# A vision state-space layer between its scans: averages folded into the sums, weights applied early, a second set of PSUM buffers

## The chip, the cores and the metric

The kernel runs on one core of a Trainium2 chip. The metric is the device time of one execution in microseconds (us). A core has five engines that take part here: TensorE (PE in the profile; PEld is its loading of weights), VectorE (DVE), ScalarE (ACT), GpSimd (POOL) and SyncE (SP), which only issues transfers. Each engine works through its own list of instructions in order and waits for the others by semaphores.

## The reference, cut to what matters

The model has four layers on an image of 2 x 56 x 56 positions with 128 channels. Layers 0 and 1 are selective-scan layers, layers 2 and 3 are attention and a mixer or experts. The change concerns layer 1 and the first step of layer 2. Layer 1 cuts the 128 channels into four heads of 32 and treats one after the other, because each head needs the result of the one before:

```python
prev = _vss_block(chunks[0], p) + vss_skip * chunks[0]
outs = [prev]
for i in range(1, g):
    s = prev + chunks[i]
    prev = _vss_block(s, p) + vss_skip * s
    outs.append(prev)
x_cat = jnp.concatenate(outs, axis=3)
x_res = cvm_skip * x_orig + x_cat
return _layernorm(x_res, final_ln_w, final_ln_b)
```

A block is `x + _ss2d(_layernorm(x))`, and `_ss2d` is, with 64 inner channels:

```python
xx, z = jnp.split(x @ p['in_proj_w'].T, 2, axis=-1)
xx = silu(depthwise_conv3x3(xx) + p['conv_b'])
# four scans over the positions: by rows, by columns, and both backwards;
# each: h = exp(dt*A)*h + dt*x*B ; y = sum over 16 states of h*C, plus x*Ds
y = y_rows + y_rows_back + y_columns + y_columns_back
y = _layernorm(y, p['out_norm_w'], p['out_norm_b']) * jax.nn.silu(z)
return y @ p['out_proj_w'].T
```

Layer 2 begins with `t = t + attention(_ln_t(t))`, a normalisation of the 128 channels of each position.

## The kernel before, in words

Two layouts are used. In "channels" layout the partitions are channels: layer 1 puts the 64 inner channels of both images side by side on 128 partitions, with 3136 positions along the free axis. In "tokens" layout 112 positions lie on the partitions; the tile `X` holds all positions and channels so. A chunk is 448 positions, four tiles of 112; there are 7 chunks (`NCH`).

**Scans.** `Scans.run` handles one head. Its order is written out by hand, step by step (`emit`). A step is one state of one quarter of the positions in one direction: ScalarE computes the decay (L334), VectorE the product `h` (L412) and the scan (L353), GpSimd the product `p` with C (L425), and TensorE adds the `p` of all 16 states into the PSUM tile `acc` (`add_up`, L373), multiplying by the identity matrix. `begin_sum` starts `acc` with the skip term (`skips`, a diagonal matrix) or with what the earlier directions left in `y`; ScalarE copies `acc` into `y` (L393).

**Between scans.** From one head to the next, and after the last, `Layer1.run` goes through the chunks. In this part the program text does not fix the order: a scheduler places the instructions of all chunks on each engine by when their inputs and buffers are free; pools give the number of buffers. For a chunk:

- `after` (the end of a head) calls `gated_tokens`: TensorE multiplies `y` by an averaging matrix into the PSUM tile `pm` (L486), VectorE subtracts it (L490), ScalarE squares (L492), GpSimd multiplies by the gate `z` (L494), TensorE forms the variance `pv` and the two output products `p1` (from the gated y) and `p2` (from the gate) (L504), ScalarE takes the root (L506), VectorE the reciprocal (L507). Then L861 and L862 combine the products, L863 on GpSimd adds the head's input, L864 adds the weighted input to give the new `prev`, and L866 adds the weighted original channels into `X`.
- `before` (the start of the next head) adds the next 32 channels to `prev` (L822), normalises (`layernorm_tokens`, L77 to L84, the last product on GpSimd), transposes on TensorE (L830), copies (L831), multiplies by the input weights (L833, L845), writes the padded image `pad` (L834) and the gate `z` with Silu (L846). `conv_rows` does the 3x3 convolution of the chunk before, on TensorE for even-numbered rows of chunks (18 matmul instructions, L455) or on VectorE (L459, L461), Silu on ScalarE (L462) and a GpSimd copy into column order (L463). At chunk 2 the first quarter of the next scans is prepared (`Scans.first`): row products, Softplus, and a way through DRAM in four transfers issued by SP.
- After the last head, `last` normalises `X` over 128 channels and applies weight and bias on GpSimd (L876), and `Attention2.chunk` normalises again (tiles `U`, `stu`), transposes for attention (L1102) and makes the value tiles (L1242).

The PSUM pool for the tiles of `after` and the transposes has one buffer per name, the one in `Attention2.start` two. ScalarE needs a table load (ACT_TABLE_LOAD) each time that its function changes among Sqrt, Silu, Exp and Softplus.

Of the kernel before, what the change touches and what calls it, by code (L numbers as in the profile page):

```python
# [21 lines left out]
B = 2  # L22
# [47 lines left out]

def layernorm_tokens(k, out, x, sq, st, d, by=None):


    nc = k.nc
    g = x.shape[1]
    mean, var = st[:, 0, :], st[:, 1, :] if by is None else by
    nc.vector.tensor_reduce(mean, x, AX.X, ALU.add)  # L77
    nc.vector.tensor_scalar_mul(mean, mean, 1.0 / d)
    nc.vector.tensor_tensor(out, x, mean.unsqueeze(2).to_broadcast([TP, g, d]), ALU.subtract)
    nc.scalar.activation(sq, out, AF.Square)  # L80
    nc.vector.tensor_reduce(var, sq, AX.X, ALU.add)
    nc.scalar.activation(var, var, AF.Sqrt, bias=k.eps[:TP], scale=1.0 / d)
    nc.vector.reciprocal(var, var)
    nc.gpsimd.tensor_tensor(out, out, var.unsqueeze(2).to_broadcast([TP, g, d]), ALU.mult)  # L84

# [20 lines left out]
class Scans:  # L106
# [263 lines left out]
    def add_up(self, x):  # L370
        nc, job, n = self.k.nc, x["job"], x["n"]
        for i in range(2):
            nc.tensor.matmul(  # L373
                job["acc"][:, i, 0:392], lhsT=self.k.ident, rhs=x["p"][:, 392 * i : 392 * (i + 1)],
                start=False, stop=n == NS - 1,
            )
# [138 lines left out]

def skips(k, pool, Ds, nch):

# [5 lines left out]
    for ci in range(nch):  # L523
        nc.vector.tensor_scalar_mul(out[:, ci], k.ident, total[:, ci : ci + 1])
    return out
# [28 lines left out]
def layer0(k, d, big, follow):  # L554
# [3 lines left out]
    with ExitStack() as ctx:  # L558
# [42 lines left out]
        with ExitStack() as sctx:  # L601
# [9 lines left out]
            sel = selection(k, wq, 1)  # L611
            skip = skips(k, wq, W["Ds"], 2)
            with k.pool("in0", 2) as ip, k.pool("pin0", 2, psum=True) as pp:
# [13 lines left out]
                "selB": lambda n: sel[:, n],  # L627
                "skip": lambda ci: skip[:, ci],
                "rows": 32,
                "rowC": 16,  # L630
# [96 lines left out]
class Layer1:  # L727
# [6 lines left out]
    def __init__(self, k, ctx, d, big):  # L734
# [20 lines left out]
        for n in ("vss_skip", "cvm_skip", "final_ln_w", "final_ln_b"):  # L755
            t = wp.tile([TP, d["L1_" + n].shape[0]], F32, name="L1" + n)
            nc.sync.dma_start(t, d["L1_" + n].partition_broadcast(TP))
            R[n] = t
        negative_exp(nc, W["A"])
        self.diag = wp.tile([128, 9, 128], F32, name="diag1")  # L760
        diagonals(k, self.diag, W["taps"])
        skip = skips(k, wp, W["Ds"].unsqueeze(2), 1)

        self.avg = wp.tile([128, 128], F32, name="avg1")
        nc.gpsimd.memset(self.avg, 0.0)
        nc.gpsimd.memset(self.avg[0:64, 0:64], 1.0 / 64)
        nc.gpsimd.memset(self.avg[64:128, 64:128], 1.0 / 64)
        self.mean = wp.tile([128, 2], F32, name="mean1")
# [4 lines left out]
        for n in ("onw", "onb"):  # L773
            t = wp.tile([128, B * D], F32, name="out" + n)
            nc.vector.tensor_scalar(t, W["out_w"], W[n], None, ALU.mult)
            self.outs.append([t])

# [5 lines left out]
        with k.pool("pinb", psum=True) as pp:  # L783
# [13 lines left out]
            "selB": lambda n: sel[:, n],  # L797
            "skip": lambda ci: skip[:, 0],
            "rows": 64,
            "rowC": 32,  # L800
# [9 lines left out]
    def before(self, head, pools, c, pad):  # L810
# [5 lines left out]
        if c < NCH:  # L816
# [9 lines left out]
            st = sp.tile([TP, 2, 4 * B], F32, name="st")  # L826
            layernorm_tokens(k, nv, sv, sq, st, D)
            pt = pp.tile([2 * D, CH], F32, name="pt")
            for i in range(4):
# [20 lines left out]
    def after(self, head, pools, c):  # L850
        k, nc, D, R = self.k, self.k.nc, self.D, self.R
        sp, pp = pools
        gate = [self.z[:, CH * c : CH * (c + 1)]]
        p1, p2, rs = gated_tokens(k, (sp, pp, sp), 1, [self.y], gate, self.avg, self.mean, *self.outs, c, B)
        t = sp.tile([TP, 4 * B, D], F32, name="t")

        def tokens(p):
            return p.rearrange("p j (b c) -> p (j b) c", c=D)

        s = self.chunk(self.prev, c)  # L860
        nc.vector.tensor_tensor(t, tokens(p1), rs.unsqueeze(2).to_broadcast([TP, 4 * B, D]), ALU.mult)  # L861
        nc.vector.tensor_tensor(t, t, tokens(p2), ALU.add)  # L862
        nc.gpsimd.tensor_tensor(t, t, s, ALU.add)  # L863
        nc.vector.scalar_tensor_tensor(s, s, R["vss_skip"], t, ALU.mult, ALU.add)  # L864
        xo = self.chunk(self.channels(head), c)
        nc.vector.scalar_tensor_tensor(xo, xo, R["cvm_skip"], s, ALU.mult, ALU.add)  # L866

    def last(self, sp, c):
# [4 lines left out]
        st = sp.tile([TP, 2, 4 * B], F32, name="stf")  # L873
        layernorm_tokens(k, xv, xv, sq, st, C)
        for op, n in ((ALU.mult, "final_ln_w"), (ALU.add, "final_ln_b")):
# [17 lines left out]
    def run(self, follow):  # L893
# [3 lines left out]
        for head in range(1, 5):  # L897
            self.scans.run()
            with ExitStack() as ctx:
                pp = ctx.enter_context(k.pool("pmid1", psum=True))  # L900
                if head < 4:
# [174 lines left out]
class Attention2:  # L1076
# [9 lines left out]
    def start(self, ctx):  # L1086
        self.sp = ctx.enter_context(self.k.pool("a2u", 2))
        self.pp = ctx.enter_context(self.k.pool("pa2", 2, psum=True))
        return self.chunk

    def chunk(self, c):
# [5 lines left out]
        flat = "p j b c -> p (j b) c"  # L1097
        layernorm_tokens(k, U.rearrange(flat), k.X[:, 4 * c : 4 * (c + 1)].rearrange(flat), sq, st, C)
        for b in range(B):
# [888 lines left out]
```

## Time and profile before

| what | us |
|---|---|
| median of 3 runs (9167.24 to 9182.95) | 9172.03 |
| profiled execution, its own time | 9196.55 |
| its span from first to last instruction | 9194.7 |
| TensorE busy in the span | 8062.6 |
| VectorE busy | 7113.2 |
| GpSimd busy | 6325.5 |
| ScalarE busy | 3845.9 |

Layer 1 lies between about 2880 and 5932 us of the span. A row of an answer gives start, length, engine, line and operation, the tiles written and read, and in square brackets the idle time before it and what ended that. A group row gives the number of instructions, the busy time and the mean length in ns. "Granted clock" is the TensorE clock in the records, 1 being full speed.

### The profile page before, as it was taken

How to read it: one execution, taken by the hardware profiler on the slowest of the kernel's cores; microseconds unless marked ns; L12 is line 12 of the kernel's file. 1: busy time of each engine (PE TensorE's matmuls, PEld its weight loads, DVE VectorE, ACT ScalarE, POOL GpSimd, SP SyncE). 2: the span in 40 equal slices, each digit the busy share in tenths (PEclk: the TensorE clock that was granted, in tenths of full speed). 3: DMA queues.
4: the chain of work that ended last, by engine and by line, in shares of the span. 5: the costliest groups of instructions: out<-in, count | busy, mean ns of one | idle time of the engine just before them, and what ended most of it. 6: DMA issues, size and time to landing. Idle time of an engine off the chain costs nothing.

```text
span 9194.7 us, 93730 instructions
## 1 busy us (share of the span) xinstructions
PE 8062.6 (88%) x28825; PEld 4797.1 (52%) x28825; DVE 7113.2 (77%) x7587; ACT 3845.9 (42%) x6551; POOL 6325.5 (69%) x4023
## 2 busy tenths in 40 slices
PE   7888888888888888888888888699999999999998
PEld 3444445444445444444444444355688888874555
DVE  8999998999996997998899799611466666665442
ACT  4555545555555555555554555234211111114331
POOL 5999996999995996997899699666311111115551
PEclk9999999999998998999999899699999999999998
DMA  5666664666663994986798599100233333320003
GB/s 155 222 220 220 222 214 129 220 220 220 221 220 102 229 225 120 223 227 157 190 227 208 136 228 227 49 3 3 71 104 101 109 93 106 95 62 7 14 5 129
DMA packets 781377, 1364.55 MB, mean 148 GB/s; under 512 B 133213, under 2 KB 406494, under 8 KB 780842
## 3 DMA queue, kind: packets, MB, share of 16 engines
q1 hardware_dynamic: 780874, 1358.56, 52.4%
q8 instruction: 228, 3.74, 0.2%
q14 instruction: 275, 2.25, 0.1%
HBM read 1318.63 MB, written 39.60 MB: 148 GB/s over the span
## 4 chain that ended last, share of the span: by engine, by line
PE 38%; DVE 11%; issue 5%; ACT 3%; POOL 2%; DMA 1%; SPq 0%; DVEq 0%; POOLq 0%; ACTq 0%
PE cv L1516 12%; PE av L1028 6%; PE sc L1034 5%; DVE h L353 5%; PE pj L1630 4%; DVE h L412 3%; PE acc L373 2%; DMA c<-rows 1%; ACT a L334 1%; PE b L161 1%; PE cv L1578 1%; PE pcv L455 1%; POOL p L425 1%; PE every L1796 1%; PE lo L969 1%
## 5 line engine op out<-in xcount | busy, mean ns | idle before, releaser
L425 POOL TENSOR_TENSOR p<-h,c 128x784 f32<-128x784 f32 x2048 | 3755.4, 1859 | 125.5 <-DVE h L353 38.6
L373 PE MATMUL acc<-p,ident 128*128 128x392 f32 x8192 | 2990.4, 499 | 23.0 <-POOL p L425 21.8
L353 DVE TENSOR_TENSOR_SCAN h<-a,state,h 128x784 f32<-128x784 f32 x1536 | 2788.5, 1837 | 48.7 <-ACT a L334 27.4
L373 PEld LDWEIGHTS acc<-p,ident 128*128 128x128 f32 x8192 | 1487.3, 193 | 1043.8 <-POOL p L425 80.4
L412 DVE TENSOR_TENSOR h<-du,b 128x784 f32<-128x784 f32 x1408 | 1332.7, 947 | 96.5 <-PE b L359 91.4
L334 ACT ACTIVATE a<-delta,L0A 128x784 f32<-128x784 f32 x1024 | 939.3, 918 | 968.5 <-DVE h L353 965.8
L334 ACT ACTIVATE a<-delta,L1A 128x784 f32<-128x784 f32 x1024 | 939.0, 917 | 918.9 <-DVE h L353 916.1
L359 PE MATMUL b<-three,sel 96*128 96x512 bf16 (+1 forms) x2816 | 730.9, 342 | 572.7 <-DVE h L412 475.6
L428 POOL TENSOR_TENSOR h<-du,b 128x784 f32<-128x784 f32 x640 | 1187.8, 1856 | 0.0
L1047 POOL TENSOR_TENSOR total<-total,e 128x448 f32<-128x448 f32 (+1 forms) x644 | 735.8, 1143 | 325.1 <-ACT e L1036 285.2
L359 PEld LDWEIGHTS <-sel 96*128 96x128 bf16 x2816 | 282.6, 100 | 1243.2 <-issue 1065.4
L353 DVE TENSOR_TENSOR_SCAN h<-a,h 128x784 f32<-128x784 f32 x512 | 900.7, 1777 | 33.7 <-ACT a L334 23.4
L1529 DVE TENSOR_TENSOR u<-u,cv 128x512 f32<-128x512 f32 x1024 | 623.4, 679 | 326.9 <-PE cv L1516 325.6
L1560 POOL TENSOR_TENSOR u<-u,S 128x1024 f32<-128x1024 f32 x64 | 150.1, 2367 | 1039.2 <-DVE S L1529 1039.2
L1036 ACT ACTIVATE e<-sc 128x448 f32<-128x448 f32 (+1 forms) x700 | 377.5, 543 | 722.8 <-PE sc L1034 594.8
L1531 ACT COPY u<-cv 128x512 f32<-128x512 f32 x256 | 149.4, 587 | 826.7 <-PE cv L1516 773.3
L1630 PE MATMUL pj<-u,Wm 128*128 128x196 f32 (+8 forms) x1536 | 351.5, 382 | 5.7 <-DVE A L1636 5.7
L1034 PE MATMUL sc<-big 128*128 128x448 f32 (+1 forms) x700 | 323.4, 548 | 12.3 <-ACT e L1036 12.3
L1028 PE MATMUL av<-e,big 128*128 128x448 f32 (+1 forms) x700 | 320.7, 545 | 1.2 <-DVE e L1041 1.1
L1610 POOL TENSOR_TENSOR both<-mpm 128x512 f32<-128x512 f32 x32 | 40.6, 1270 | 395.0 <-DVE Wm L1666 271.5
L1630 PEld LDWEIGHTS pj<-u,Wm 128*128 128x128 f32 x1536 | 266.6, 191 | 70.4 <-issue 45.7
L973 DVE TENSOR_REDUCE m<-lo 112x1 f32<-112x448 f32 x392 | 229.2, 617 | 95.4 <-PE lo L969 95.1
(438 smaller groups left out, 10866.9 us busy)
## 6 DMA issues: line engine op xcount, KB each, us to landing
c<-rows SPq DMA_DIRECT2D x1024, 392.0 KB, 4.0
c<-rows SPq DMA_DIRECT2D x2048, 196.0 KB, 4.8
b<-rows SPq DMA_DIRECT2D x320, 392.0 KB, 4.5
b<-rows SPq DMA_DIRECT2D x640, 196.0 KB, 4.6
H<-raw SPq DMA_DIRECT2D x32, 1568.0 KB, 7.6
wC<-win SPq DMA_DIRECT2D x64, 576.0 KB, 6.2
w<-in_L_weight_dram SPq DMA_DIRECT2D x52, 512.0 KB, 5.3
wA<-win SPq DMA_DIRECT2D x64, 384.0 KB, 5.5
```

Of the source, the lines that this page charges most:

```text
L334: self.k.nc.scalar.activation(x["a"], g["delta"][ci], AF.Exp, scale=self.w["A"](g["kd"], ci, x["n"]))
L353: self.k.nc.vector.tensor_tensor_scan(h, a, h, start, ALU.mult, ALU.add)
L359: self.k.nc.tensor.matmul(ps[:, c0:c1], lhsT=self.w["selB"](x["n"]), rhs=x["g"]["three"][:, c0:c1], start=True, stop=True)
L373: nc.tensor.matmul(job["acc"][:, i, 0:392], lhsT=self.k.ident, rhs=x["p"][:, 392 * i : 392 * (i + 1)], start=False, stop=n == NS - 1,)
L412: nc.vector.tensor_tensor(one["h"], one["g"]["du"][one["ci"]], one["b"], ALU.mult)
L425: nc.gpsimd.tensor_tensor(now["p"], now["h"], now["c"], ALU.mult)
L428: nc.gpsimd.tensor_tensor(three["h"], three["g"]["du"][three["ci"]], three["b"], ALU.mult)
L1028: nc.tensor.matmul(acc, lhsT=V[b][:n, j, :], rhs=e[:n], start=j == 0, stop=j == NKT - 1)
L1034: nc.tensor.matmul(ps[:n], lhsT=keys[b][:, KT * j : KT * j + n], rhs=q, start=True, stop=True)
L1047: nc.gpsimd.tensor_tensor(total[:n], total[:n], e[:n], ALU.add)
L1516: self.k.nc.tensor.matmul(ps[:, b], lhsT=v[:, C * b : C * (b + 1)], rhs=h, start=i == 0, stop=i == len(terms) - 1)
L1630: nc.tensor.matmul(ps[:, lo - c0 : hi - c0], lhsT=Ws[f][:, eo, r, :], rhs=u[:, b, f, lo - a0 : hi - a0], start=f == 0, stop=f == 1,)
```

## The change

- The matrix by which layer 1 adds `p` into `acc` is no longer the identity but the identity minus the averaging matrix (`center`); `skips` for layer 1 is a multiple of it too. `y` then comes out of the scans with its channel average already taken off. `after` no longer calls `gated_tokens` and has no `pm`.
- `before` multiplies the 32 channels in `X` by `cvm_skip` and `prev` by `vss_skip` plus 1 on GpSimd, once their unweighted values are used. `after` then only adds: u = p2 + s, t = p1 * rs, s = t + u, and x += s on GpSimd (for the last head u += x on GpSimd and x = t + u).
- `p1` and `p2` share one PSUM tile `p`, and its pool has two buffers per name in `Layer1.run`; the pool in `Attention2.start` has four.
- In `last` and in `Attention2.chunk` the product by the reciprocal root moves from one GpSimd instruction to eight ScalarE instructions, one for each block of 128 channels.

```diff
@@ layernorm_tokens @@
-    nc.gpsimd.tensor_tensor(out, out, var.unsqueeze(2).to_broadcast([TP, g, d]), ALU.mult)
+    if last == "POOL":
+        nc.gpsimd.tensor_tensor(out, out, var.unsqueeze(2).to_broadcast([TP, g, d]), ALU.mult)
+    else:
+        for i in range(g):
+            nc.scalar.activation(out[:, i], out[:, i], AF.Copy, scale=var[:, i : i + 1])
@@ Scans.add_up @@
-                job["acc"][:, i, 0:392], lhsT=self.k.ident, rhs=x["p"][:, 392 * i : 392 * (i + 1)],
+                job["acc"][:, i, 0:392], lhsT=self.w["sum"], rhs=x["p"][:, 392 * i : 392 * (i + 1)],
@@ Layer1.__init__ @@
+        nc.vector.tensor_scalar_add(R["vss_skip"], R["vss_skip"], 1.0)
...
-        self.avg = wp.tile([128, 128], F32, name="avg1")
...
+        nc.gpsimd.memset(center[64:128, 64:128], 1.0 / 64)
+        nc.vector.tensor_tensor(center, k.ident, center, ALU.subtract)
+        skip = skips(k, wp, W["Ds"].unsqueeze(2), 1, center)
@@ Layer1.before @@
             layernorm_tokens(k, nv, sv, sq, st, D)
+            nc.gpsimd.tensor_scalar(xs, xs, self.R["cvm_skip"], None, ALU.mult)
+            nc.gpsimd.tensor_scalar(sv, sv, self.R["vss_skip"], None, ALU.mult)
@@ Layer1.after @@
-        gate = [self.z[:, CH * c : CH * (c + 1)]]
-        p1, p2, rs = gated_tokens(k, (sp, pp, sp), 1, [self.y], gate, self.avg, self.mean, *self.outs, c, B)
+        y, gate = self.y[:, cs], self.z[:, cs]
+        sq = sp.tile([128, CH], F32, name="sq0")
+        nc.scalar.activation(sq, y, AF.Square)
+        yz = sp.tile([128, CH], F32, name="yc0")
+        nc.gpsimd.tensor_tensor(yz, y, gate, ALU.mult)
+        p = pp.tile([TP, 2, 4, B * D], F32, name="p")
+        pv = pp.tile([TP, 4 * B], F32, name="pv")
...
+        for i, ts in enumerate(tiles):
+            nc.tensor.matmul(p[:, 1, i], lhsT=gate[:, ts], rhs=self.outs[1], start=True, stop=True)
+        for i, ts in enumerate(tiles):
+            nc.tensor.matmul(pv[:, B * i : B * (i + 1)], lhsT=sq[:, ts], rhs=self.mean, start=True, stop=True)
+        for i, ts in enumerate(tiles):
+            nc.tensor.matmul(p[:, 0, i], lhsT=yz[:, ts], rhs=self.outs[0], start=True, stop=True)
+        rs = sp.tile([TP, 4 * B], F32, name="rs")
+        nc.scalar.activation(rs, pv, AF.Sqrt, bias=k.eps[:TP])
+        nc.vector.reciprocal(rs, rs)
...
+        nc.vector.tensor_tensor(u, p2, s, ALU.add)
+        if head == 3:
+            nc.gpsimd.tensor_tensor(u, u, x, ALU.add)
         t = sp.tile([TP, 4 * B, D], F32, name="t")
...
-        nc.vector.tensor_tensor(t, tokens(p1), rs.unsqueeze(2).to_broadcast([TP, 4 * B, D]), ALU.mult)
-        nc.vector.tensor_tensor(t, t, tokens(p2), ALU.add)
-        nc.gpsimd.tensor_tensor(t, t, s, ALU.add)
-        nc.vector.scalar_tensor_tensor(s, s, R["vss_skip"], t, ALU.mult, ALU.add)
-        xo = self.chunk(self.channels(head), c)
-        nc.vector.scalar_tensor_tensor(xo, xo, R["cvm_skip"], s, ALU.mult, ALU.add)
+        nc.vector.tensor_tensor(t, p1, rs.unsqueeze(2).to_broadcast([TP, 4 * B, D]), ALU.mult)
+        if head == 3:
+            nc.vector.tensor_tensor(x, t, u, ALU.add)
+        else:
+            nc.vector.tensor_tensor(s, t, u, ALU.add)
+            nc.gpsimd.tensor_tensor(x, x, s, ALU.add)
@@ Layer1.last @@
-        layernorm_tokens(k, xv, xv, sq, st, C)
+        layernorm_tokens(k, xv, xv, sq, st, C, last="ACT")
@@ Layer1.run @@
-                pp = ctx.enter_context(k.pool("pmid1", psum=True))
+                pp = ctx.enter_context(k.pool("pmid1", 2, psum=True))
@@ Attention2.start @@
-        self.pp = ctx.enter_context(self.k.pool("pa2", 2, psum=True))
+        self.pp = ctx.enter_context(self.k.pool("pa2", 4, psum=True))
@@ Attention2.chunk @@
-        layernorm_tokens(k, U.rearrange(flat), k.X[:, 4 * c : 4 * (c + 1)].rearrange(flat), sq, st, C)
+        x = k.X[:, 4 * c : 4 * (c + 1)].rearrange(flat)
+        layernorm_tokens(k, U.rearrange(flat), x, sq, st, C, last="ACT")
```

## The prediction, made before the changed kernel ran

> **What bounds the kernel now.** I read the table of stretches first, because the edit touches only the work between two runs of scans. During scans VectorE and GpSimd are 96 to 99% busy and nothing there changes except the name of a 128x128 weight. So I took, for each gap, the time from the end of the last scan (L353) to the start of the next one, or to the last copy of V, from the instruction timeline, and asked for the busy time inside it.
>
> ```profile
> core 0: us, PE busy (x) PEld busy (x) DVE busy (x) ACT busy (x) POOL busy (x), PEclk, DMA share, GB/s
> 3545.60:3657.50 111.90, 97.53 (x334) 56.39 (x334) 53.01 (x115) 58.51 (x88) 33.77 (x37) 0.77 0.12 28
> 4295.30:4401.60 106.30, 93.28 (x334) 53.23 (x333) 53.52 (x116) 58.60 (x88) 34.29 (x37) 0.81 0.13 29
> 5040.60:5152.50 111.90, 97.59 (x334) 56.25 (x334) 53.04 (x115) 58.50 (x88) 33.53 (x37) 0.77 0.12 27
> 5790.30:5932.00 141.70, 72.29 (x306) 55.25 (x306) 103.91 (x154) 37.26 (x65) 82.92 (x47) 0.57 0.02 6
> 2761.00:2906.30 145.30, 128.44 (x548) 80.98 (x548) 74.83 (x139) 77.08 (x115) 45.51 (x52) 0.89 0.13 33
> ```
>
> Read the first column against the others. The first three rows are the gaps between heads (110.0 us on average): TensorE shows 93 to 98 us of work, but at a granted clock of 0.77 to 0.81; no other engine is over 59. Those gaps are a chain that passes from engine to engine. The fourth row, after the last head, is different: TensorE half idle, VectorE 104 us and GpSimd 83 us of 141.7. The fifth is the gap before head 0, which shares its time with the end of the first layer.
>
> Then the chain that ended last, inside the fourth row:
>
> ```profile
> 5816.86 2.78 POOL X L84
> 5819.70 2.41 POOL X L876
> 5822.19 2.34 POOL X L876
> 5824.53 1.10 POOL yc L494
> 5825.67 0.64 PE p L504 x2
> ```
>
> GpSimd works alone here: product with 1/sigma, weight, bias, and only then the gate product of another chunk, for which TensorE waits. By line the chain of that row gives L84 17.6% and L876 17.6% of 143 us, so 25.1 us for the product alone.
>
> Third, the timeline of ScalarE in a gap between heads:
>
> ```profile
> 3621.95 1.28 ACT L82 ACT_TABLE_LOAD   x1
> 3623.24 0.30 ACT L82 ACTIVATE st<-st,eps 112x8 f32<-112x8 f32 x1
> 3623.56 1.28 ACT L462 ACT_TABLE_LOAD   x1
> 3624.85 0.63 ACT L462 ACTIVATE big<-pcv,L1conv_b 128x448 f32<-128x448 f32 x1
> 3626.44 1.28 ACT L506 ACT_TABLE_LOAD   x1
> 3627.73 0.27 ACT L506 ACTIVATE rs<-pv,eps 112x8 f32<-112x8 f32 x1
> 3628.54 1.28 ACT L846 ACT_TABLE_LOAD   x1
> 3629.84 0.63 ACT L846 ACTIVATE pair<-pcv,inb 128x448 f32<-128x448 f32 x1
> ```
>
> Four of the 20 table loads of this gap. Each starts 0.02 us after its predecessor, its activation follows 0.01 to 0.02 us behind it, and the chain passes through this stretch: ScalarE is the late engine here, and half of its time goes to switching between Sqrt, Silu and Exp.
>
> Last, the groups that price what moves (GpSimd over the whole run; VectorE L866 in the last gap, then in the first gap between heads; the columns are busy us, mean ns):
>
> ```profile
> L863 POOL TENSOR_TENSOR t<-t,pair 112x256 f32<-112x256 f32 x28 | 25.2, 899 | 71.2 <-DVE t L862 60.2 <-DVE st L83 11.0
> L84 POOL TENSOR_TENSOR nrm<-nrm,st 112x256 f32<-112x256 f32 x28 | 19.2, 685 | 81.0 <-DVE st L83 72.9 <-DVE st L78 8.1
> L84 POOL TENSOR_TENSOR X<-X,stf 112x1024 f32<-112x1024 f32 x7 | 15.9, 2265 | 16.0 <-DVE stf L83 15.9
> L84 POOL TENSOR_TENSOR U<-U,stu 112x1024 f32<-112x1024 f32 x7 | 13.3, 1905 | 15.1 <-DVE stu L83 15.1
> ...
> L866 DVE SCALAR_TENSOR_TENSOR X<-X,L1cvm_skip,pair 112x256 f32<-112x256 f32 x7 | 7.9, 1130 | 0.0
> ...
> L866 DVE SCALAR_TENSOR_TENSOR X<-X,L1cvm_skip,pair 112x256 f32<-112x256 f32 x7 | 4.4, 627 | 0.0
> ```
>
> ```profile
> L834 ACT ACTIVATE pad<-pcv,inb 128x448 f32<-128x448 f32 x28 | 17.7, 634 | 16.3 <-PE pcv L833 16.2
> L80 ACT ACTIVATE sq<-nrm 112x256 f32<-112x256 f32 x28 | 11.6, 414 | 27.1 <-DVE nrm L79 27.1
> L80 ACT ACTIVATE squ<-U 112x1024 f32<-112x1024 f32 x7 | 7.4, 1057 | 19.2 <-DVE U L79 19.2
> ```
>
> **Part 1, averages folded into the sums.** Each chunk loses two instructions on `pm` (L486) and the subtraction L490. In the gaps between heads the chain has 9.2% of 113 us on `pm`, 10.4 us; the 7 subtractions are 4.3 us. The square now reads y directly and the gate product starts with it. The `acc` matmuls keep shape, count and operand type: no change in the scans. The setup has one more 128x128 subtraction (about 0.2 us) under the first layer's end: nothing.
>
> **Part 2, weighting ahead of use.** VectorE per chunk: L861, L862, L864, L866 (0.42+0.42+0.48+0.48) become u, t, s (3 x 0.42); with L490 that is 1.2 us less, 8 us per gap. GpSimd swaps L863 for x+=s and gets two tensor_scalar of 112x256 per chunk, 56 in all. No row shows that instruction. The nearest are its neighbour `nrm` (0.685 mean) above it and, below, the page "GPSIMD Engine Reference" of the Trainium skill, section "3.1 Elementwise — side-by-side cycle accounting": at best 1.8 cycles an element with one input, an estimate of 256 x 1.8 / 1.2 GHz = 0.38 us. I take 0.62, near the row; a contended one may be 0.9, as L863's mean. That is 8.7 us per gap on an engine with 34 of 110 used. But GpSimd runs in order: in the changed order the first `nrm` product stands behind all seven gate products, three x+=s, two weightings of X and two of prev (before: three gate products and three L863). Whoever waits for it is the transpose and everything after.
>
> **Part 3, two PSUM buffers and a new order.** With the banks doubled the scheduler issues both products of five chunks and all variances before the first transpose, and groups the Sqrt work: the changed program has 14 table loads per gap where it had 21 (one lies past the first scan), none fewer elsewhere (293 against 314). Here the row and the Trainium skill differ. The rows above show 1.28 us a switch and no more, so 7 are 9.0 us per gap. "ScalarE: Activation LUTs", "What ACT_TABLE_LOAD costs", adds a drain of about 1.38 us, 2.66 a switch, which would make it 18.6. I take the row.
>
> Now a gap between heads, in us from the last scan's end, from the changed order and these durations (eight small matmuls 1.3 to 1.5, as in this gap at the low clock):
> - GpSimd's last products and the copies out end at 6.9, as before. Gate products 8, 9.1; TensorE 8.1 to 13.8 for chunks 0 and 1, then both products and variances to about 29. GpSimd's seventh gate product waits for chunk 4's matmuls (28.1). First `nrm` product done at 30; before 28.2 (3573.19 + 0.62). Slightly later: the wait in order.
> - Transposes, hT, in-projections, rest of the products: first convolution at 41; before 42.3 (3587.85). It ends at 49.6.
> - From here ScalarE sets the pace: pad row 54.8, two table loads, Silu 58.9, both row copies 62, Softplus 66, pad 66.5; second convolution 66.6 to 74 (before 69.5). The band copies fill 67 to 72, because ScalarE waits in order for their DMAs (5.1 us after the row copy, as before) and for GpSimd; the SP order is unchanged. Third convolution 83.3 (before 87.2), fourth 94 (before 100.5), and 2.9 + 8 to the first scan: 105.
> So of 10.4 + 4.3 + 9.0 us taken away about 5 us arrive (110.0 to 105); the rest goes into the wait for the first `nrm` and the serial ScalarE part. Three gaps: -15, with 0 to -14 for each.
>
> **Part 4, last gap.** The two L84 products leave GpSimd: 25.1 us of its chain. `pm` goes too, 3.3% of 143, 4.7 us. They become 16 activations of 112x128 per chunk, which no row shows. From L80 at 256 and 1024 elements: 0.835 ns an element over a start of 0.20; L834 with a pointer operand has a start of 0.26; successive ones overlap by 0.11. So 0.26 each, 2.1 us per product, against 1.9 and 2.27 on GpSimd. The same ScalarE page states 280 ns + 0.833 N less 93 of overlap, an estimate of 0.294, 2.35 per product: by it, part of a chunk's own latency speaks against the move. Over 7 chunks that is 29 or 33 us on an engine with 37 of 142 used; it becomes 67 to 70, still under VectorE. VectorE loses 8 us of instructions and part of its collisions: L866 took 1.13 here against 0.63 between heads. 83 - 29 = 54 on GpSimd, about 91 on VectorE, which begins at 8, waits some 10 while the first chunks go round, and leaves a tail of 6: 115. Four banks for transposes and V tiles take small waits from TensorE. 25.1 + 4.7, less 2.1 at the first product and at the last, is 26. I take -27; VectorE's 104 as bound gives -15, no waits at all -40.
>
> **Part 5, gap before head 0.** It gets 14 weightings, 9 us on GpSimd with 45 of 145 used, ordered between the first layer's gate products: +2, from -1 to +8.
>
> **Sum:** -15 - 27 + 2 = -40. The profiled execution took 9196.55 (span 9194.7 and 1.85 around it), so 9156 for one like it; the median of the runs is 24.5 lower, 9172.03, and the forecast 9132.
>
> **Rivals.**
> (a) Only the last gap gains: between heads the order of GpSimd and the row-to-bands chain give all back. For it: `nrm` is later in my walk and one gap took 106.3 already. -27 + 2 = -25: 9147.
> (b) More: ScalarE is what the chain waits for, so all 9 us of table loads and part of `pm` come through, -14 per gap, and the last gap falls to 102, -40: -80, 9092. For it: in the gap at 3545 the chain crosses six table loads.
> (c) The last gap is VectorE's already (104 busy): -12, between heads nothing, +4 ahead of head 0: -8, 9164.
> (d) Slower: the weightings on GpSimd are dear. All 56 stand in order ahead of products that a transpose waits for. At 0.62 they are in the sum; each 0.1 more costs up to 5.6 us. From 0.62 + 40/56 = 1.33 us the gain is gone, from 1.65 it is slower by over 0.2%; at 2.2, 9220. Against: no 112x256 row of GpSimd has a mean over 0.9.
> That the change doesn't do what it says is excluded by its order: `pm` is gone and the loads are counted.
>
> **How the numbers follow.** My case 0.46 (-25 to -60, own range 9112 to 9147), (b) 0.22, (a) 0.16, (c) 0.11, (d) 0.05. About 18 us, 0.2%, is what a measurement of this kernel can tell from no change. Faster 0.46 + 0.22 + 0.16 = 0.84, same 0.11, slower 0.05. The range takes in (a), most of (b) and the near half of (c): 9080 to 9162.
>
> **What would show it.** Last gap near 115 with L876 on GpSimd without an L84 between; the new activations at 0.26 apart; three gaps near 105 with 13 or 14 table loads; tensor_scalar near 0.62; scans unchanged. I am wrong if the gaps between heads stay at 110, if the weightings exceed 1.3 us, or if the scans' `acc` matmuls or the granted clock move.

## The result, and the profile after

The changed kernel takes 9141.9 us (median of 6 runs, 9138.3 to 9148.5). The kernel before took 9179.6 us beside it (6 runs). That is 37.7 us less by the medians (0.41%). The ratio of the runs, taken side by side, is 0.9956, with a 95% interval of 0.9947 to 0.9966: 0.44% faster. The forecast was 9132 with a range of 9080 to 9162. The profiled execution took 9148.52 us (span 9146.7), 48 us less than that of before.

The net agrees with the forecast of -40. Its terms do not, and the rest of this text is about that. Of the signs that the prediction named, the order on GpSimd and the number of table loads came true, and the sizes did not: the last gap, the gaps between heads, the spacing of the new activations and the time of a weighting. Here is the same table of stretches for the kernel after: three gaps between heads, the last gap up to the last copy of V, and the gap before head 0. Columns are the length, then busy us of TensorE, of its weight loads, of VectorE, ScalarE and GpSimd, then granted clock, DMA share and GB/s.

```profile
3550.60:3648.00 97.40, 88.02 (x320) 55.63 (x319) 43.94 (x101) 49.37 (x81) 44.84 (x50) 0.77 0.13 32
...
5754.20:5881.90 127.70, 67.79 (x292) 51.92 (x292) 85.48 (x140) 68.99 (x177) 51.91 (x33) 0.56 0.02 7
2762.20:2914.60 152.40, 131.65 (x548) 83.72 (x548) 74.64 (x141) 77.41 (x115) 58.60 (x66) 0.87 0.13 31
```

The first gap between heads went from 111.9 to 97.4 us at the same granted clock, 0.77. The last went from 141.7 to 127.7. The gap before head 0 grew from 145.3 to 152.4.

One profile is not enough for the split, because the granted clock moves these gaps. I profiled both kernels a second time (in the last group of experiments). In us, with the last gap taken here and below up to the memset of the filter table P that ends it (2.4 us before the mark used above):

```
                        before        changed        mean change   forecast
before head 0           145.3, 140.1  152.4, 153.8      +10.4         +2
three between heads     330.1, 316.5  294.3, 292.1      -30.1        -15
last gap                139.3, 136.8  125.1, 126.1      -12.4        -27
four stretches of scans 2553.9, 2553.1  2545.3, 2550.5   -5.6          0
sum                                                     -37.7        -40
```

That the means add up to the difference of the medians is in part chance: the profiled spans of the two kernels differ by 35.8 us in the mean, and the two profiles of one kernel by up to 6 us in a stretch, by 13.6 in the three gaps of the kernel before together. The signs of the four rows, and that the three gaps between heads gain more than the last gap, do not hang on this.

The next groups price the new instructions over the whole run (busy us, mean ns of one, idle time before them):

```profile
L837 POOL TENSOR_SCALAR X<-X,L1cvm_skip 112x256 f32<-112x256 f32 x28 | 27.8, 994 | 25.6 <-DVE pair L829 13.5 <-DVE pair L831 7.1 <-DVE st L84 4.9
L838 POOL TENSOR_SCALAR pair<-pair,L1vss_skip 112x256 f32<-112x256 f32 x28 | 27.8, 995 | 23.1 <-DVE nrm L80 23.1
L86 POOL TENSOR_TENSOR nrm<-nrm,st 112x256 f32<-112x256 f32 x28 | 19.7, 708 | 17.0 <-DVE st L84 16.6
...
L907 POOL TENSOR_TENSOR X<-X,L1final_ln_w 112x1024 f32<-112x1024 f32 x7 | 16.5, 2353 | 35.3 <-ACT X L89 35.3
```

A weighting takes 0.995 us in the mean and 0.92 in the median, not 0.62: more than the two-operand product of the same shape in the third row. The fourth row shows where the last gap's new wait stands: GpSimd now waits 35.3 us for the ScalarE products.

ScalarE in the last gap, around the first of those products (start, us, instruction, idle before):

```profile
5791.30 1.86 ACT L89 ACTIVATE X<-X,stf 112x128 f32<-112x128 f32 x6 [1.01 <-DVE stf L84]
5793.07 1.04 ACT L81 ACTIVATE squ<-U 112x1024 f32<-112x1024 f32 x1
5794.01 0.68 ACT L89 ACTIVATE X<-X,stf 112x128 f32<-112x128 f32 x2
...
5797.29 2.46 ACT L89 ACTIVATE U<-U,stu 112x128 f32<-112x128 f32 x8 [0.94 <-DVE stu L84]
```

Six activations in 1.86 us and eight in 2.46 are 0.30 apart, where I had 0.26. The estimate of 0.294 from the Trainium skill ("ScalarE: Activation LUTs", "What ACT_TABLE_LOAD costs") was the better one. The second row shows a cost that I left out: another chunk's square, 1.04 us, stands between the sixth and the seventh, so the chunk's product is complete 3.4 us after it began.

### The profile page after: what moved, and what is told of

Same layout as the page of the kernel before. It is cut to its first block, busy times and chain, and to the rows that moved or that the text cites. A ratio compares the mean times of both kernels' runs of the same rounds, so it can differ in the third digit from the quotient of the medians.

```text
span 9146.7 us, 93661 instructions
## 1 busy us (share of the span) xinstructions
PE 8045.3 (88%) x28769; PEld 4798.2 (52%) x28769; DVE 7065.7 (77%) x7533; ACT 3851.1 (42%) x6642; POOL 6343.6 (69%) x4065
## 4 chain that ended last, share of the span: by engine, by line
PE 46%; DVE 26%; issue 14%; ACT 7%; POOL 4%; DMA 2%; SPq 1%; DVEq 0%; POOLq 0%; ACTq 0%
DVE h L358 13%; PE cv L1548 13%; DVE h L417 8%; PE av L1059 6%; PE sc L1065 5%; PE acc L378 4%; PE pj L1662 4%; ACT a L339 3%; PE b L166 3%; PE pcv L460 2%; DMA c<-rows 1%; PE b L364 1%; POOL p L430 1%; POOL h L433 1%; PE acc L392 1%
## 5 line engine op out<-in xcount | busy, mean ns | idle before, releaser
L378 PE MATMUL acc<-p,center 128*128 128x392 f32 x4096 | 1500.8, 500 | 16.0 <-POOL p L430 14.9
L378 PE MATMUL acc<-p,ident 128*128 128x392 f32 x4096 | 1494.3, 499 | 6.1 <-POOL p L430 6.0
L378 PEld LDWEIGHTS acc<-p,center 128*128 128x128 f32 x4096 | 742.9, 193 | 529.3 <-POOL p L430 50.7
L378 PEld LDWEIGHTS acc<-p,ident 128*128 128x128 f32 x4096 | 745.4, 193 | 512.7 <-issue 26.8
```

The lines of the kernel that those rows point to most:

```text
L378: nc.tensor.matmul(job["acc"][:, i, 0:392], lhsT=self.w["sum"], rhs=x["p"][:, 392 * i : 392 * (i + 1)], start=False, stop=n == NS - 1,)
```

## Experiments

Each group was timed on one chip, with the kernel before beside it. Gaps are from each run's profile, those between heads as the mean of three. Medians of different groups are less well comparable than ratios within one.

### Group 1: one part undone, or one part alone

Part 4 undone:

```diff
-layernorm_tokens(k, xv, xv, sq, st, C, last="ACT")
+layernorm_tokens(k, xv, xv, sq, st, C)
...
-layernorm_tokens(k, U.rearrange(flat), x, sq, st, C, last="ACT")
+layernorm_tokens(k, U.rearrange(flat), x, sq, st, C)
```

> The changed kernel with the two 112x1024 products of the last gap back on GpSimd (part 4 undone, four PSUM banks kept). Theory A, the move is worth the wait it takes away from GpSimd (25.1 us of L84 in the chain before, less about 2 x 2.3 for the first and last product): the last gap goes from 127.7 us back to 138 to 148, the total up by 10 to 20. Theory B, the move only traded one wait for another (GpSimd waits 35.3 us for the new activations in the last gap) and the 14 us gained there came from the averages and the smaller epilogue: the last gap stays within 3 us of 127.7. Both: the gaps between heads unchanged at 97 to 100.

Measured: 9146.7 us, ratio 0.9970 (0.9956 to 0.9983). Last gap 135.1, between heads 97.2, before head 0 144.7. Part 4 is worth 10.0 us of the last gap (135.1 against 125.1): at the lower end of theory A's 10 to 20, much more than theory B's 3. The total rose by 4.8 us only, not by theory A's 10 to 20, because another stretch fell: the two kernels have the same instructions up to the last gap, and yet the gap before head 0 is 144.7 here and 152.4 there. I come back to that.

Part 3 undone between heads and in the last gap:

```diff
-pp = ctx.enter_context(k.pool("pmid1", 2, psum=True))
+pp = ctx.enter_context(k.pool("pmid1", psum=True))
```

> The changed kernel with one PSUM buffer a name instead of two between heads and in the last gap (part 3 undone). The order of ScalarE's instructions has 12 table loads in a gap between heads (changed kernel 14, before 21). Theory A, the prediction's: the doubled banks let the products of all chunks run ahead, and the gaps between heads need them: they go from 97 to 100 back to 104 to 108 us. Theory B, the gain of 12 us a gap is the averages' (no product to wait for at the head of each chunk, and with it the switches of table), the banks are worth little: gaps 95 to 100, total within 5 us of the changed kernel.

Measured: 9159.9 us, ratio 0.9983 (0.9974 to 0.9991). Between heads 102.0, last gap 125.0, before head 0 159.1. The gaps between heads lie between both theories: the second buffer gives about 4 us in each, nothing in the last gap. It is not through table loads, since this kernel has two fewer of them per gap and is slower. Of the 18 us on the changed kernel (by the medians), 12 are these gaps and 7 the gap before head 0, whose instructions are the same, in the same order. The other half of part 3, the four buffers of `Attention2.start`, was never undone by itself.

Part 2 undone:

```diff
-nc.gpsimd.tensor_scalar(xs, xs, self.R["cvm_skip"], None, ALU.mult)
-nc.gpsimd.tensor_scalar(sv, sv, self.R["vss_skip"], None, ALU.mult)
...
-nc.vector.tensor_tensor(u, p2, s, ALU.add)
+nc.vector.scalar_tensor_tensor(u, s, R["vss_skip"], p2, ALU.mult, ALU.add)
 if head == 3:
-    nc.gpsimd.tensor_tensor(u, u, x, ALU.add)
+    nc.vector.scalar_tensor_tensor(u, x, R["cvm_skip"], u, ALU.mult, ALU.add)
...
-    nc.gpsimd.tensor_tensor(x, x, s, ALU.add)
+    nc.vector.scalar_tensor_tensor(x, x, R["cvm_skip"], s, ALU.mult, ALU.add)
```

> The changed kernel without the two weightings on GpSimd: the factors are applied in the epilogue again, by VectorE instructions of two operations (prev times its factor plus the product, X times its factor plus the sum), the rest as changed; GpSimd also loses x+=s. Theory A, the weightings at 0.925 us, in order ahead of the first layer's gate products, made the gap before head 0 7.1 us longer: it falls from 152.4 to 145 to 147, and the gaps between heads (17 us of weightings and x+=s off GpSimd, 3 us more on VectorE) fall by 0 to 3 from 97 to 100: total 7 to 15 under the changed kernel. Theory B, the weightings lie beside other work and the longer gap before head 0 is due to the changed order alone: it stays at 150 to 153, and the added VectorE work makes the gaps between heads up to 3 us longer: total 0 to 9 over it.

Measured: 9125.8 us, ratio 0.9943 (0.9926 to 0.9959). Before head 0 146.0, between heads 95.2, last gap 122.9. Theory A holds: every gap is shorter than in the changed kernel. The rows show what the factor of `prev` costs VectorE, here in a gap between heads, first the changed kernel, then this one:

```profile
L888 DVE TENSOR_TENSOR u<-p,pair 112x256 f32<-112x256 f32 x7 | 2.9, 413 | 18.9 <-PE p L881 18.9
```

```profile
L886 DVE SCALAR_TENSOR_TENSOR u<-pair,L1vss_skip,p 112x256 f32<-112x256 f32 x7 | 3.3, 468 | 12.8 <-PE p L879 12.8
```

The factor rides along in an instruction that is there anyway: 55 ns more, against 0.92 us and more on GpSimd. The wait ahead of it also falls, from 18.9 to 12.8 us. The factor of X takes an instruction of its own (L895, 571 ns in the mean) in place of a weighting and an addition on GpSimd. In all, VectorE is busy 46.2 us in this gap instead of 43.9, GpSimd 25.7 instead of 44.8.

Part 1 alone, on the kernel before:

```diff
-job["acc"][:, i, 0:392], lhsT=self.k.ident, rhs=x["p"][:, 392 * i : 392 * (i + 1)],
+job["acc"][:, i, 0:392], lhsT=self.w["sum"], rhs=x["p"][:, 392 * i : 392 * (i + 1)],
...
-        nc.vector.tensor_tensor(yc, y[ci][:, cs], pm, ALU.subtract)
+        yn = y[ci][:, cs]
+        if avg is not None:
+            nc.vector.tensor_tensor(yc, yn, pm, ALU.subtract)
+            yn = yc
...
-        nc.scalar.activation(s, yc, AF.Square)
+        nc.scalar.activation(s, yn, AF.Square)
...
-        nc.gpsimd.tensor_tensor(yc, yc, gate[ci], ALU.mult)
+        nc.gpsimd.tensor_tensor(yc, yn, gate[ci], ALU.mult)
```

Layer 1 hands over `None` for `avg`, so its product into `pm` falls away too.

> The kernel before with part 1 alone: the channel average is taken off in the scans' sums, pm and the subtraction are gone from the second layer's epilogue, everything else as before (one PSUM buffer, weights in the epilogue, last products on GpSimd). ScalarE's order has 15 table loads in a gap between heads instead of 21. Theory A, as predicted: of what leaves, most goes into other waits, and the grouping of the Sqrt work needs the doubled banks: gaps between heads 105 to 110 us. Theory B, the averages carry the gaps between heads: 97 to 102. In the last gap, A and B: 141.7 less 4.7 for pm, 135 to 139; gap before head 0 unchanged at 145.

Measured: 9172.7 us, ratio 0.9996 (0.9987 to 1.0005): no difference in the total. Between heads 104.7, last gap 144.9, before head 0 143.7. Between heads it lies at the edge of theory A's 105 to 110: 5.3 us below the first profile of before, at a like granted clock (0.76 to 0.77 here, 0.77 to 0.81 there), and 0.8 below the second (0.82 to 0.85). The last gap became longer, against both theories. These are VectorE's subtractions of the mean in it, before and then here:

```profile
L79 DVE TENSOR_TENSOR X<-X,stf 112x1024 f32<-112x1024 f32 x7 | 10.6, 1513 | 0.0
L79 DVE TENSOR_TENSOR U<-X,stu 112x1024 f32<-112x1024 f32 x7 | 9.9, 1417 | 0.0
```

```profile
L79 DVE TENSOR_TENSOR U<-X,stu 112x1024 f32<-112x1024 f32 x7 | 12.4, 1765 | 0.0
L79 DVE TENSOR_TENSOR X<-X,stf 112x1024 f32<-112x1024 f32 x7 | 12.2, 1747 | 0.0
```

Same instructions, 4.1 us more in sum: five of the 14 took 1.9 to 3.4 us behind a GpSimd instruction that had begun before them, two in the kernel before. So part 1 alone loses in the last gap part of what it gains between heads. These rows do not explain the loss, though: VectorE's busy time in that gap fell from 103.3 to 100.1 us and GpSimd's rose from 81.4 to 85.4. Its cause stays open.

### Group 2: what sets the last gap now

All four start from the late-weights kernel (last gap 122.9). First the two halves of part 4, one product back on GpSimd each:

> The late-weights kernel (last gap 122.9 us) with the first of the two last-gap products, X times 1/sigma, back on GpSimd; U times 1/sigma stays on ScalarE. Theory A, ScalarE's queue is what the last gap waits for (GpSimd 35.3 us for the X activations, the transposes 31.9 for the U ones, in the changed kernel): with half the activations off it the gap falls, to 112 to 119. Theory B, GpSimd's big instructions set it, because they also hold up VectorE's two-operand work: with 16 us more on GpSimd (45 to 61) it rises to 126 to 131, half of the way back to the 135 of both products on GpSimd. Gaps between heads unchanged at 94 to 96; gap before head 0 anywhere from 139 to 155 with the granted clock 0.95 to 0.83 (this stretch has the same instructions as the late-weights kernel).

> The late-weights kernel with the second product, U times 1/sigma, back on GpSimd, X times 1/sigma on ScalarE. Theory A (ScalarE's queue): 112 to 119 as for the other half. Theory B (GpSimd's share): 126 to 131. If the two halves differ, the one that is better on ScalarE is U, whose transposes can start after two of its eight activations, while X has to be complete for the weight instruction behind it: then this one is the worse.

Measured: X on GpSimd 9137.6 us, ratio 0.9957 (0.9942 to 0.9972), last gap 129.6. U on GpSimd 9129.4 us, ratio 0.9950 (0.9935 to 0.9965), last gap 128.8. Theory B holds for both: each half costs 6 to 7 us, and taking half of the activations off ScalarE brings nothing. VectorE's busy time rises from 88.1 to 100.5 and 98.9 us, though its instructions stay the same. The 35.3 us that GpSimd waits for ScalarE were not the bound. That U's half would be the worse one, as the second text had it, did not come true.

Then the opposite, the final weight and bias taken off GpSimd as well, both, or the weight only:

```diff
-nc.gpsimd.tensor_tensor(xv, xv, self.R[n].unsqueeze(1).to_broadcast([TP, 4 * B, C]), op)
+nc.vector.tensor_tensor(xv, xv, self.R[n].unsqueeze(1).to_broadcast([TP, 4 * B, C]), op)
```

```diff
-nc.gpsimd.tensor_tensor(xv, xv, self.R[n].unsqueeze(1).to_broadcast([TP, 4 * B, C]), op)
+e = nc.vector if op == ALU.mult else nc.gpsimd
+e.tensor_tensor(xv, xv, self.R[n].unsqueeze(1).to_broadcast([TP, 4 * B, C]), op)
```

> The late-weights kernel with the final weight and bias products (two of 112x1024 per chunk, 2.35 us each on GpSimd) on VectorE, where a 112x1024 instruction takes 1.2 us. GpSimd goes from 45 to 12 us in the last gap, VectorE from 88 to 88 + 14 x 1.2 less what it loses of waiting beside GpSimd's instructions (128x1 products of 1.2 us, L894 of 1.0 us against 0.42). Theory A, the last gap is a chain through GpSimd and the hold-ups it causes: 105 to 115. Theory B, VectorE's own work sets it once it has to do more: 123 to 132.

> As the one before, but with the weight on VectorE and the bias on GpSimd. Theory A (chain through GpSimd): between 122.9 and the gap of the one before, 113 to 119. Theory B (VectorE sets it): 122 to 128. Half of the hold-ups stay.

Measured: 9123.5 us, ratio 0.9944 (0.9929 to 0.9959), last gap 122.2; and 9125.9 us, ratio 0.9944 (0.9928 to 0.9961), last gap 122.2. Theory A fails, and the first of the two lies 0.8 below its theory B's 123 to 132, the second at the lower end of 122 to 128. With GpSimd down from 44.7 to 12.3 us of the gap its length stays:

```profile
5735.83:5858.08 122.25, 67.56 (x288) 51.96 (x288) 95.48 (x160) 68.74 (x176) 12.33 (x11) 0.56 0.02 6
```

VectorE took over 14 instructions of 1.22 us, 17 us in all, and its busy time rose by 7.4 only. From 26 to 114 us of this gap it pauses once for more than 1 us (1.2), and is busy 82 of 88 us. That speaks for VectorE as the engine that sets the gap in this kernel; no run tries it by taking work off VectorE.

What GpSimd does to VectorE is seen in instructions of one element a partition. First the kernel with part 4 undone (both products on GpSimd), then the one with weight and bias on VectorE, both in the last gap:

```profile
L80 DVE TENSOR_TENSOR X<-X,stf 112x1024 f32<-112x1024 f32 x7 | 13.8, 1975 | 0.0
...
L1389 DVE TENSOR_TENSOR hard<-hard,free 128x1 f32<-128x1 f32 x4 | 6.2, 1556 | 0.1
```

```profile
L80 DVE TENSOR_TENSOR X<-X,stf 112x1024 f32<-112x1024 f32 x7 | 8.5, 1210 | 0.0
...
L1387 DVE TENSOR_TENSOR hard<-hard,free 128x1 f32<-128x1 f32 x4 | 0.6, 159 | 0.1
```

1556 ns in the mean against 159 for the same 128x1 product, 1975 against 1210 for the subtraction. The single instructions show what happens, here in the kernel with part 4 undone:

```profile
5862.84 2.19 DVE L1389 TENSOR_TENSOR hard<-hard,free 128x1 f32<-128x1 f32 x1
```

```profile
5848.99 3.32 POOL L907 TENSOR_TENSOR X<-X,L1final_ln_b 112x1024 f32<-112x1024 f32 x1
5862.67 2.34 POOL L907 TENSOR_TENSOR X<-X,L1final_ln_b 112x1024 f32<-112x1024 f32 x1
```

The 128x1 product began 0.17 us behind the start of a GpSimd instruction (the last row) and ended 0.02 us after its end. Of the other three of its kind two took 1.75 and 2.19 us in the same way, and one 0.11 with GpSimd idle. In this gap every subtraction of 112x1024 that began behind a GpSimd instruction ended 1.08 us after that one's end, and every `x = t+u` 0.28 us after it. Where VectorE began first it was not held (1.17 us for a subtraction, 0.37 for `x = t+u`), and the GpSimd instruction behind it became longer instead: 3.2 to 3.3 us for a final weight or bias (the first row of GpSimd above), 2.34 otherwise. So on these instructions the two engines work one at a time, and whichever comes second waits for the other's whole instruction.

It is not every instruction. In the changed kernel's last gap `x = t+u` (L894, both inputs in SBUF) took 0.41 to 0.43 us four times and 0.66, 2.21 and 2.55 behind GpSimd, 1014 ns in the mean; `t` and `u` of the same shape, with one input from PSUM, took 0.37 to 0.43 also where GpSimd was busy throughout; the sums over 112x1024, with one input, stay at 1.21 us. An exception with one input is the 112x8 product by a constant (L79): 1.90 and 1.03 us behind GpSimd in the kernel with part 4 undone, 0.16 otherwise. The Trainium skill says the same of the rule ("GPSIMD Engine Reference", "1. Specifications": GpSimd's way to SBUF is shared with VectorE, which collides with it in instructions with two SBUF inputs, and in a mode that uses two ports); no run here shows whether L79 is in that mode.

With part 4 undone GpSimd is busy 81.8 us in the last gap and VectorE 100.2; with it they are 50.4 and 84.9. In the chain that ended last, added up by engine over this gap, GpSimd's part goes from 44.5 to 25.8 us and ScalarE's from 0.8 to 16.9, so the moved products nearly change places; VectorE's part goes from 45.6 to 35.3, TensorE's from 36.2 to 40.2. By this account part 4 gains its 10 us not from the 25 us of GpSimd's chain, but from VectorE's instructions that no longer wait. It is a reading of two profiles; no run has the one effect without the other.

### Group 3: both kernels again, and the candidates

> The changed kernel once more, nothing altered, beside the two candidates. Theory A: the 7.1 us that the gap before head 0 grew in its first profile are mostly the granted clock. Three runs with the same instructions there gave 144.7 us with TensorE busy 122.8, 152.4 with 131.65, 159.1 with 138.0, so 0.95 us for each: the gap will be 144.7 + 0.95 x (busy - 122.8) within 2 us, whatever its length. Theory B: the weightings ahead of the first layer's gate products cost it 7 us of themselves: 151 or more at any clock. Gaps between heads 97 to 100, last gap 124 to 126.

> The late-weights kernel again, timed with the changed kernel on one chip. Its gaps added up 3 x 2.9 between heads, 2.2 in the last and about 3.5 at equal clock before head 0 less than the changed kernel's: 9125 to 9132 if that kernel takes 9142, so 10 to 17 us under it. If only the first profile was lucky: within 5 us of it.

> The late-weights kernel with the final weight and bias on VectorE again. Theory B held in the last gap (122.2 against 122.9): so within 4 us of the late-weights kernel, and 10 to 18 us under the changed kernel.

> The kernel before once more, for the scatter of its own stretches. Its four stretches of scans took 638.5 us each in the first profile, those of the kernels derived from it 633.5 to 642.4 with the same number of instructions. Theory A, that is scatter of waits and no effect of the change: one or more of the four will now fall below 637. Theory B, the change shortens them by 2 us each: all four at 637.5 to 640 again. Gaps between heads 106 to 112, last gap 138 to 142.

Measured: the changed kernel 9144.8 us, ratio 0.9957 (0.9943 to 0.9970), last gap 126.1. The late-weights kernel 9118.2 us, ratio 0.9928 (0.9915 to 0.9940). The one with the affine on VectorE 9126.0 us, ratio 0.9936 (0.9924 to 0.9949), last gap 120.9. The kernel before 9169.1 us in a single run.

The late-weights kernel beats the changed one: the intervals do not overlap, and it is 26.6 us below it here (16 us below by the medians of the earlier groups). That is more than the 10 to 17 expected. Taking the final weight and bias off GpSimd on top of it brings nothing to the total: it lies 7.8 us above the late-weights kernel, where within 4 was expected.

For the gap before head 0, the rows of the changed kernel and of the kernel with part 4 undone, which have the same instructions in it:

```profile
2757.77:2911.55 153.78, 132.81 (x548) 83.24 (x548) 76.36 (x142) 77.38 (x115) 58.10 (x67) 0.87 0.13 31
```

```profile
2762.08:2906.78 144.70, 122.80 (x548) 76.25 (x548) 76.30 (x141) 77.03 (x115) 58.41 (x66) 0.93 0.13 33
```

The formula of theory A gives 144.7 + 0.95 x 10.0 = 154.2 for the first; it took 153.8. That alone would have fitted theory B too; what speaks against "151 or more at any clock" is the second row. So with the same instructions in the same order the length follows the granted clock. The weightings cost something as well: at TensorE busy 128.4 the same line gives 150.0, and the late-weights kernel took 145.6 and 146.0 at 128.4 to 128.5, the kernel before 145.3. All ten profiles without weightings lie 2.6 to 4.8 us under the line. So the weightings cost 3 to 5 us at equal clock, between the theories. The rest of the +10.4 is the clock: 0.83 to 0.93 in four runs with weightings, 0.89 to 0.94 in ten without. Whether the weightings lower it is open. That a clock gate looks at TensorE's activity in windows that run on regardless of the kernel, so that equal code can meet different clocks, is what the Trainium skill states ("TensorE: Matmul & The Clock Gate", Part 1); the scatter here fits that, and no run here shows the windows.

For the scans' stretches, none of the four of before fell below 637.0 us the second time (637.1 to 641.3), which speaks for theory B, if narrowly: three lie within 0.6 of the line, and of the 48 stretches of the other profiles 29 lie below all eight of before. The other profiles average 635.6 to 637.6 each, the two of before 638.5 and 638.3. The stretches hold the same number of instructions to within a few, so it is waits that differ, by about 2 us a stretch. The cause was not tried.

## Why the prediction was right, and where only its sum was

**Gaps between heads: -15 forecast, -30 measured.** The first half of the walk was near: first `nrm` product done at 31.5 us (forecast 30), first convolution from 43.7 (41), Softplus done at 69.2 (66), second convolution 67.1 to 74.1 (66.6 to 74). The second convolution's time was luck: it was to follow its newest row, and that row was written at 69.1 to 69.7, inside it. The step that failed is "Third convolution 83.3 (before 87.2), fourth 94 (before 100.5)". They started at 78.6 and 89.0. TensorE, before and then after, in the first of these gaps:

```profile
3630.94 1.86 PE L833 MATMUL pcv<-big,L1in_w 64*128 64x448 f32 x2 [2.19 <-ACT big L831]
3632.73 8.47 PE L455 MATMUL pcv<-pad,diag 128*128 128x448 f32 x18
...
3643.28 1.02 PE L833 MATMUL pcv<-big,L1in_w 64*128 64x448 f32 x2 [0.63 <-ACT big L831]
3644.13 0.91 PE L845 MATMUL pcv<-big,L1in_w 64*128 64x448 f32 x2
3646.06 8.62 PE L455 MATMUL pcv<-pad,diag 128*128 128x448 f32 x18 [1.02 <-ACT pad L834]
3654.52 0.50 PE L359 MATMUL b<-three,sel 96*128 96x512 bf16 x2
3656.08 0.49 PE L359 MATMUL b<-three,sel 96*128 96x512 bf16 x2 [1.06 <-DVE h L412]
```

```profile
3628.24 1.02 PE L844 MATMUL pcv<-big,L1in_w 64*128 64x448 f32 x2
3629.19 7.06 PE L460 MATMUL pcv<-pad,diag 128*128 128x448 f32 x18
3636.18 1.02 PE L856 MATMUL pcv<-big,L1in_w 64*128 64x448 f32 x2
3637.13 0.51 PE L364 MATMUL b<-three,sel 96*128 96x512 bf16 x2
3637.91 1.02 PE L844 MATMUL pcv<-big,L1in_w 64*128 64x448 f32 x2 [0.27 <-ACT big L467]
3638.76 0.91 PE L856 MATMUL pcv<-big,L1in_w 64*128 64x448 f32 x2
3639.65 7.03 PE L460 MATMUL pcv<-pad,diag 128*128 128x448 f32 x18
3646.52 0.50 PE L364 MATMUL b<-three,sel 96*128 96x512 bf16 x2
```

Before, an in-projection of the late chunks waited for the copy of the transposed chunk (`big`, L831) ahead of each convolution, 2.19 and 0.63 us. After, that wait is gone, since the late chunks are normalised earlier: the transposes of the last two begin 75.0 us after the last scan, where before they began at 82.6 and 96.5. And I had the third convolution wait for its newest row of the padded image. ScalarE shows when that row came:

```profile
3631.19 1.28 ACT L467 ACT_TABLE_LOAD   x1
3632.49 0.67 ACT L467 ACTIVATE big<-cv,L1conv_b 128x448 f32<-128x448 f32 x1
3633.06 0.62 ACT L845 ACTIVATE pad<-pcv,inb 128x448 f32<-128x448 f32 x1
```

It was written at 3633.06 to 3633.68, inside the convolution of 3629.19 to 3636.25. Only the taps on the newest row have to wait: the 13th of the 18 matmuls is the first of them, and it began at 3633.81. The kernel before already did so: its third convolution began at 3632.73, and the newest row came at

```profile
3632.83 0.64 ACT L834 ACTIVATE pad<-pcv,inb 128x448 f32<-128x448 f32 x1 [0.15 <-PE pcv L833]
```

Both late convolutions also took 7.0 us instead of 8.5, at a higher granted clock, first before and then after:

```profile
3632.73:3641.20 8.47, 8.47 (x20) 4.04 (x19) 5.07 (x12) 3.92 (x5) 1.62 (x2) 0.83 0.05 11
```

```profile
3629.19:3636.25 7.06, 7.06 (x20) 3.31 (x19) 3.56 (x6) 6.97 (x8) 1.02 (x1) 1.00 0.69 165
```

And the first scan followed 1.3 us after the fourth convolution, not 2.9, since the first of the two products `b` that it needs now stands ahead of that convolution (3637.13). Start, length and tail of the fourth convolution make up the 7.6 us between the forecast of 105 and the 97.4 of this gap.

**Part 1 and part 3.** "With the banks doubled the scheduler issues both products of five chunks ... 14 table loads per gap where it had 21" gave the credit to the wrong part. Part 1 alone already has 15 loads, and one buffer with the rest has 12. A load is 1.28 us in the rows above, with the activation 0.02 us behind it, as the row said and not with a further drain of 1.38. (In the prediction's rows of ScalarE other instructions, of L846, L831 and L834, stand between those printed; that each load starts right behind its predecessor is so with them.) But fewer loads do not of themselves mean a shorter gap: 15 loads 104.7 us, 12 loads 102.0, 14 loads 98.1. Along this row of kernels part 1 gives 5 us a gap by the first profile of before and 1 by the second, the new epilogue with early weights 3, the second buffer 4.

**Part 2.** The term was 0.62 us each; it measured 0.92 to 0.995. Rival (d) had the right sign for this part; whether its slope, up to 5.6 us for each 0.1, was right no run shows, as none changes the time of a weighting alone. By the late-weights kernel all 56 weightings with the additions after them cost 16 to 27 us of the total, net of what VectorE does in their place, and the changed kernel is faster in spite of them.

**Part 4: -27 forecast for the last gap, -12 measured.** The busy times came out near the forecast: GpSimd 52 (54), ScalarE 69 (67 to 70), VectorE 85 (91). The step that failed is the last one, "begins at 8, waits some 10 while the first chunks go round, and leaves a tail of 6: 115". VectorE is idle for 40 of 125.1 us, not 24. What it waits for, in the last gap of the changed kernel (us in total, times, longest):

```profile
DVE stu L78 <- POOL X L907: 12.2, 4, 4.5
DVE u L888 <- PE p L881: 9.8, 3, 7.2
DVE big L64 <- PE pt L1134: 6.3, 7, 2.7
```

It starts on the first chunk at 11.1 us. The last chunk alone takes 16.4 us after VectorE's last 1/sigma but one, nearly all of it in single file: weight and bias on GpSimd, sum, subtraction, square, 1/sigma, eight activations, transposes, copies. To add a bound and a guess for its waits was not enough; the last chunk's latency has to be walked as the first one's was. GpSimd's share of the chain, 25.1 us, was not what taking it off would give either. The half-way kernels put that at 6 to 7 us for each product. And what VectorE no longer loses to waiting was in the sum with about 5 us (104 - 8 - 91); it measured about 10 (103.3 - 8 - 84.9).

**Part 5: +2 forecast, +10 in the mean.** The bound of +8 holds for what the weightings themselves do (3 to 5); the granted clock was not in the sum. That it might move stood among the signs of being wrong, and in this gap it did: 0.89 and 0.94 before, 0.87 in both profiles of the changed kernel.

**Sum.** A gain that was 15 us too small, one 15 us too large, a loss 8 too small and 6 us in the scans that no step has: the forecast stood because these cancel, and that is luck. What it had right beyond the sum is which stretches gain and which loses.

## What to carry to other kernels

A factor that can ride in a two-operation instruction of VectorE costs tens of ns there; as an instruction of its own on GpSimd it cost 0.92 us and a place in an in-order queue. Work taken off a busy GpSimd is to be priced also by what VectorE's instructions with two SBUF inputs gain (about 15 us of busy time in the last gap here), and the last item of a pipeline by its whole latency. And before a gap is explained, look at the granted clock in its row: the same stretch with the same 548 matmuls took from 144.7 to 159.1 us here, at 0.93 to 0.83.

## What was not expected of the hardware

On GpSimd a one-operand product by a scalar of each partition (112x256) took 0.92 us, the two-operand product of that shape 0.62 at its fastest. On VectorE a 128x1 product took 0.11 to 0.16 us with GpSimd idle and 1.75 to 2.34 behind a 112x1024 instruction of GpSimd, with which it ended; the reductions of 112x1024 (1.21 us) did not change.
